# An edge-gated graph layer on one core: ScalarE's copies emitted ahead of the gate, and the low part of one product formed on TensorE

## Chip, core and metric

One core of a Trainium2 chip runs the whole layer in one launch. The metric is the device time of that launch in microseconds (us). The profile names the engines PE (TensorE; PEld is its weight load), DVE (VectorE), ACT (ScalarE), POOL (GpSimd) and SP (SyncE); the same names are used here.

## The reference, cut to what matters

```
B, C, D = 16, 1024, 256                       # batches, nodes, features
pre_u  = x @ W1[:D];  pre_v = x @ W1[D:]
S[b,u,v] = sigmoid( relu(pre_u[b,u] + pre_v[b,v] + b1) @ W2 + b2 )
a[b,v] = sum over u of S[b,u,v] * adj[u,v] * x[b,u]
m[b,v] = (sum over u of adj[u,v] * x[b,u]) * x[b,v]
z = beta1*x + beta2*(a @ Wa + ba) + beta3*(m @ Wm + bm)
```

`adj` is sparse (a few edges per node), so the kernel works edge by edge and not on the full square of nodes.

## The kernel before, in words

**Blocks and steps.** Batches are taken four at a time (four groups g), nodes v in tiles of 128 (eight tiles vt). A pair (g, vt) is a block; there are 32 blocks k, the last eight of them being the fourth group. A block has T = 10 steps s, two windows of 64 nodes with five steps of 128 edges each; step n is 10k + s, and there are 320. `table[g]` in DRAM holds, for each node u, `pre_u` and x of the group's four batches, 2048 numbers in all.

**What a step does.** `fetch` (L518, POOL queue) gathers 128 rows of the table into one of eight `fetched` buffers. `expand(n)` (L607, PE) spreads `pre_v + b1` of the block, held in `X`, over the 128 edges by two matmuls into `pc` (PSUM, two buffers). `add(n)` (L639, DVE) adds `pc` to the fetched `pre_u`. `gate(n)` (L647, DVE) makes relu and the product with W2 with its sum, four times, one for each batch; then ACT makes the sigmoid `gt` (L650) and four scaled copies `left` (L652), beside `left_adj` (L617). `aggregate(n)` (L664, PE) multiplies `left` with the fetched x and sums into `acc`. It is emitted two or three steps later, for two steps at once, in odd steps.

**What a block does beside it.** `products(n, k, s)` emits, by the step's number s in the block: `rows` (L459 to L465: `pre_u` for the table of a later group, with an ACT copy and an SP store); `turn_over` (L674: four transposes L682 of `ev`, an ACT copy L685 to `LT`, later the DVE product L696); `block_end` (L701: the last products L713 of the block before, in s = 4 to 7, an ACT copy L718 to `z` in s = 5 and 7, and a step later the DVE addition L719 and its store); and `halves` (L473) of the next block in s = 1, 3, 4, 6, 7. `halves` splits `pre_v + b1` in two parts that a reduced float32 (`FR`) can hold: ACT copies the PSUM tile `p` twice, to `X` rounded (L482) and to `low` whole (L483); DVE subtracts (L484); ACT writes the difference and a second copy of the high part into the free halves of `X` (L486, L489).

All products, transposes and `p` share one PSUM pool, `misc`, of two buffers: a third use waits until ACT has copied the one two before.

**The order is written by hand** (`manual_schedule`): each engine's queue runs in the order in which the loop from L860 emits. For n from ROOM = 10 on, a step emits: the aggregates that are due (with ACT's copy of a finished `acc` to `ev`, L672), the next `mark` (L550), `add(n+1)`, `gate(n)`, `left_adj(n+1)`, `do(n)`, `expand(n+2)`, the load of x for the output, `fill(n, False)`, `products(n)`. `do(n)` emits what was put off to step n by `after`: DVE's L484, L696 and L719, and SP's stores. `fill` emits one piece of the edge lists of later tiles (`lists`, ended by step 110). So on ACT the order in a step is

```
ev, mark, gt(n), left(n) x4, left_adj(n+1), copies of products(n)
```

and on PE it is aggregates, `expand(n+2)`, products(n).

Of the kernel before, what the change touches and what calls it, by code (L numbers as in the profile page):

```python
# [7 lines left out]
FP = mybir.dt.float32  # L8
FR = mybir.dt.float32r
I32 = mybir.dt.int32  # L10
AF = mybir.ActivationFunctionType
ALU = mybir.AluOpType
AX = mybir.AxisListType
P = 128
# [3 lines left out]
def kernel(  # L18
# [42 lines left out]
    nc = tc.nc  # L61
    B, N, D = x.shape
    NT = N // P
    DC = D // P
    GB = 4
    NG = B // GB
    GD = GB * D
    W = 64
    NW = P // W
# [31 lines left out]
    def fixed(shape, name, dt=FP):  # L101
        return const.tile(shape, dt, name=name)
# [9 lines left out]
    upto = fixed([P, E], "upto")  # L112
# [3 lines left out]
    row = rows32[:, 0:1]  # L116
# [56 lines left out]
    slot_of = fixed([P, NW, TW], "slot_of")  # L173
    for w in range(NW):
        nc.vector.tensor_scalar(slot_of[:, w, :], upto[:, :TW], float(P), row, ALU.mult, ALU.add)
    ident = fixed([P, P], "ident")
    nc.vector.tensor_scalar(ident, upto[:, :P], row, None, ALU.is_equal)
    place = upto[:, :W].rearrange("p (q v) -> p q v", v=V)
    slot, nth = upto, upto[:, :S]

# [11 lines left out]
    b1_p = fixed([P, D], "b1_p", FR)  # L192
# [16 lines left out]
    big = main.enter_context(tc.tile_pool(name="big", bufs=2))  # L209
# [10 lines left out]
    def small(name):  # L220
        return psm.tile([P, 512], FP, name="misc")
# [180 lines left out]
    def after(step, f):  # L402
        due.setdefault(step, []).append(f)
# [5 lines left out]
    order = [(g, vt) for some in (range(FIRST), range(FIRST, NT)) for g in range(2) for vt in some]  # L409
    again = [(g, vt) for g, vt in order if vt >= FIRST or g == 1]  # L410
    order += [(g, vt) for g in range(2, NG) for vt in range(NT)]
    hTs = {}
# [29 lines left out]
    def half_product(p, hT, wt, h, begun):  # L442
        for bb in range(2):
            for i in range(DC):
                nc.tensor.matmul(p[:, bb * D:(bb + 1) * D], hT[:, 2 * h + bb, i, :], wt[:, i, :],  # L445
                                 start=(i == 0 and not begun), stop=(i == DC - 1), skip_group_check=begun)

    def add_row(p, parts):
        nc.tensor.matmul(p, unit, parts.unsqueeze(1).to_broadcast([P, 2, D]),  # L449
                         start=True, stop=False, skip_group_check=True)  # L450
# [19 lines left out]

    cuts = {}

    def halves(k):  # L473
        X = cuts[k] = big.tile([P, NW, GD], FR, name="X")
        low = one.tile([P, GD], FP, name="low")
        for h in range(2):
            step = yield
            c = slice(2 * h * D, (2 * h + 2) * D)
            p = small("p")
            add_row(p, b1_p)  # L480
            half_product(p, hTs[order[k]], w_v, h, True)
            nc.scalar.copy(X[:, 0, c], p)  # L482
            nc.scalar.copy(low[:, c], p)  # L483
        after(step + (2 if k else 1), lambda: nc.vector.tensor_tensor(low, low, X[:, 0, :].bitcast(FP), ALU.subtract))  # L484
        yield
        nc.scalar.copy(X[W:, 1, :], X[W:, 0, :].bitcast(FP))  # L486
        for w in range(NW):
            yield
            nc.scalar.copy(X[(1 - w) * W:(2 - w) * W, w, :], low[w * W:(w + 1) * W])  # L489
# [5 lines left out]
    def do(step):  # L495
        for f in due.pop(step, ()):
            f()
# [8 lines left out]
    T = TW * NW  # L506

    BS = NG * NT

    def where(n):  # L510
        k, s = divmod(n, T)
        w, j = divmod(s, TW)
        return k, *order[k], w, j
# [20 lines left out]
    w_v = load_weights(W1[D:2 * D], "w_v", nc.sync)  # L534
# [11 lines left out]
    marks, pcs, accs, evs, hbs, LTs, lefts = {}, {}, {}, {}, {}, {}, {}  # L546
# [12 lines left out]
    parts = halves(0)  # L559
# [42 lines left out]
    def expand(n):  # L602
        k, g, vt, w, j = where(n)
        pcs[n] = psc.tile([P, GD], FP, name="pc")
        for h in range(2):
            c = slice(2 * h * D, (2 * h + 2) * D)
            nc.tensor.matmul(pcs[n][:, c], marks[n // TW][:, j * P:(j + 1) * P], cuts[k][:, w, c],  # L607
                             start=True, stop=True)
# [22 lines left out]
    def fill(n, gap=True):  # L631
        for r in running:
            if r[1] == gap and r[2] <= n:
                piece_of(r, n)
                break

    def add(n):
        t = fetched[at_slot[n]][:, :GD]
        nc.vector.tensor_tensor(t, t, pcs.pop(n), ALU.add)  # L639

    def gate(n):
        m = len(QUARTERS[n % TW])
# [157 lines left out]
    def products(n, k, s):  # L800
        nonlocal end, parts
        made_rows(n)
        if (s == 2 and 0 < k < BS) or n == total:
            turn_over(k - 1, 1, 1, n)
        z = 3 if n < ROOM else 4
        if z <= s < z + 4 and 0 < k < BS:
            if s == z:
                end = block_end(k - 1)
                next(end)
            go(end, n)  # L810
        if ROOM <= n < total - T:
            if s in (8, 9):
                turn_over(k, 0, s - 8, n)
        elif s == 7 and k < BS:
            turn_over(k, 0, 0, n)
        if s == 7 and k == BS - 1 or s == 8 and n < ROOM:
            turn_over(k, 0, 1, n)
        if (s == 0 and 0 < k < BS) or n == total - 1:
            turn_over(k - (s == 0), 1, 0, n)
        if n == total - 2:  # L820
            end = tail(tails[:2], n)
            next(end)
        elif n == total - 1:
            go(end, n)
        elif n >= total:
            end = tail([tails[2 + n - total]], n)
            next(end)
            go(end, n)
            go(end, n)
        later = n >= ROOM  # L830
        if k + 1 < BS and s - later in (0, 2, 3, 5, 6):
            if s == later:
                parts = halves(k + 1)
                next(parts)
            go(parts, n)

# [3 lines left out]
    total = BS * T  # L840
    ROOM, MORE, LISTS = 10, 3, 110
    ahead = NF
    add(0)

    def refill():
# [14 lines left out]
    for n in range(total + 2):  # L860
        k, s = divmod(n, T)
        if n < total - 3:
            last_in = n - 1 if n % 2 or n < ROOM else done
        else:
            last_in = n
        while done < min(last_in, total):
            gather_in(done)
            done += 1
        if n % TW == 1 and n // TW + 1 < total // TW:
            load_mark(n // TW + 1)  # L870
        if n < ROOM:
            if n + 2 < total:
                expand(n + 2)
            products(n, k, s)
        if n + 1 < total:
            add(n + 1)
        if n < total:
            gate(n)
            if n + 1 < total:
                left_adj(n + 1)  # L880
        do(n)
        if n >= ROOM and n + 2 < total:
            expand(n + 2)
        if n == 1:
            w_a = load_weights(Wa, "w_a", nc.sync)
            w_m = load_weights(Wm, "w_m", nc.sync)
            bias = load_rows(bm, D, "bias", nc.sync, spare[:, 1])
            ba_b = load_rows(ba, D, "ba_b", nc.sync, spare[:, 2])
            be1 = load_rows(beta1, 1, "be1", nc.sync)
            be2 = load_rows(beta2, 1, "be2", nc.sync)  # L890
            be3 = load_rows(beta3, 1, "be3", nc.sync)
            after(10, scale_late)
        if s in (5, 7) and k < BS - 1:
            h = s // 7
            hb = big.tile([P, 2, D], FP, name="h_blk", bufs=4)
            hbs.setdefault(k, []).append(hb)
            g, vt = order[k]
            nc.sync.dma_start(hb.rearrange("p b d -> p (b d)"),
                              table[g][vt * P:(vt + 1) * P, GD + 2 * h * D:GD + (2 * h + 2) * D])
        if n == total - 6:  # L900
            hbs[BS - 1] = hT_free.pop(0).rearrange("p b c n -> p b (c n)")
            for v, m, f in tails:
                for h, o in tail_rows(x, v, m, f):
                    nc.sync.dma_start(h, o)
        for i in advance.get(n, ()):
            next(made[i], None)
        if n in start_list:
            running.append([made[start_list[n]], True, n])
            piece_of(running[-1], n)
        fill(n, False)  # L910
        if n >= ROOM:
            products(n, k, s)
        if n == LISTS:
            assert not running and all(next(x, None) is None for x in made)
            lists_done()
            more = main.enter_context(tc.tile_pool(name="more", bufs=1))
            hT_free.extend(hT_places(more, MORE, NH))
        if n == 120:
            nc.gpsimd.partition_all_reduce(longest, rest, P, bass_isa.ReduceOp.max)
            after(n + 12, count_rest)  # L920
# [7 lines left out]
    with tc.If(any_left > 0):  # L928
        with ExitStack() as s2:
# [4 lines left out]
            for vt in range(NT):  # L934
# [55 lines left out]
                for b in range(B):  # L990
# [7 lines left out]
                    for k, w in enumerate((w_m, w_a)):  # L998
                        for c in range(DC):
                            nc.tensor.matmul(pz, lt[:, k, c, :], w[:, c, :],  # L1000
                                             start=(k == 0 and c == 0), stop=(k == 1 and c == DC - 1))
# [34 lines left out]
```

## Time and profile before

| | us |
|---|---|
| three runs | 1098.24, 1101.68, 1102.35 (median 1101.68) |
| profiled execution, device time | 1101.12 |
| its span, first to last instruction | 1099.3 |
| PE, DVE, ACT busy | 1022.2, 1025.4, 872.5 |
| add of step 10 to add of step 120 (blocks 1 to 11) | 101.4 to 483.3: 34.7 a block |
| add of step 120 to add of step 230 (blocks 12 to 22) | 483.3 to 819.5: 30.56 a block |
| add of step 230 to add of step 310 (blocks 23 to 30) | 819.5 to 1050.4: 28.86 a block |

The stages are read from the starts of the additions L639 in the timeline: there are 320, one a step. "Busy" of PE counts a matmul until its modelled end; consecutive matmuls overlap, and the chain of waits is the better guide to what a matmul takes in a stream. The number after an "idle before" or in the list of waits is time in which an engine stood, and the name behind the arrow is what let it go on.

### The profile page before, as it was taken

Reading aid. Unit: us, or ns where it says so; the run is one execution under the profiler, and the core shown is the slowest. Engines: PE = TensorE matmul, PEld = TensorE weight load, DVE = VectorE, ACT = ScalarE, POOL = GpSimd, SP = SyncE. Lnnn points to the kernel's source line nnn. Section 1 sums busy time; section 2 is a strip of 40 time slices with the busy share of each in tenths; the row PEclk is TensorE's granted clock in tenths of the full one; section 3 lists DMA queues with packets and bytes.
Section 4 is the critical chain, followed back from the end, with each engine's and each line's share of the span. In section 5 each row is a group of like instructions: output and inputs, shape, how many; then the busy total and the mean of one; then the engine's idle time right before and its main releaser. Section 6 shows DMA issues by size and latency. Waiting matters only on the chain.

```text
span 1099.3 us, 23917 instructions
## 1 busy us (share of the span) xinstructions
PE 1022.2 (93%) x7645; PEld 726.5 (66%) x7645; DVE 1025.4 (93%) x3487; ACT 872.5 (79%) x2616; POOL 464.3 (42%) x453
## 2 busy tenths in 40 slices
PE   7777889999899999999999999999999999999986
PEld 6654556776667666676777677767766666666653
DVE  8788888898999999999999999999999999999994
ACT  3347667787778888888988889888889888888873
POOL 2746575445347433563334343433343333333330
PEclk9988989999899999999999999999999999999999
DMA  9999799999999999999999999999999999999991
GB/s 285 331 391 311 295 327 303 356 394 382 384 343 344 391 410 381 384 378 396 408 382 400 406 400 398 386 398 388 353 362 383 372 350 357 359 372 363 354 335 42
DMA packets 149030, 394.54 MB, mean 359 GB/s; under 512 B 18224, under 2 KB 96048, under 8 KB 112688
## 3 DMA queue, kind: packets, MB, share of 16 engines
q0 software_dynamic: 50240, 300.11, 69.6%
q1 hardware_dynamic: 85360, 79.71, 22.9%
q10 hardware_dynamic: 13296, 13.11, 3.6%
q8 instruction: 62, 1.02, 0.3%
q14 instruction: 72, 0.59, 0.1%
HBM read 396.93 MB, written 50.33 MB: 407 GB/s over the span
## 4 chain that ended last, share of the span: by engine, by line
PE 39%; DVE 32%; issue 10%; ACT 9%; DMA 6%; POOL 2%; another core or an unknown queue 0%; SPq 0%; POOLq 0%; DVEq 0%; ACTq 0%
DVE fetched L647 15%; DVE fetched L639 12%; PE acc L664 10%; PE misc L713 10%; PE misc L445 7%; PE pc L607 7%; ACT left L652 3%; PE misc L682 2%; DMA hT<-in_xT_dram 2%; DMA hT<-in_x_dram 2%; PE misc L449 1%; DMA fetched<-table,uidx 1%; DVE low L484 1%; DVE h_blk L719 1%; DVE LT L696 1%
## 5 line engine op out<-in xcount | busy, mean ns | idle before, releaser
L518 POOL DMA_INDIRECT fetched<-table,uidx x320 | 345.5, 1080 | 540.9 <-PE acc L664 384.1
L647 DVE SCALAR_TENSOR_TENSOR fetched<-fetched,w_b 128x256 f32<-128x256 f32 x1280 | 476.5, 418 | 0.0
L639 DVE TENSOR_TENSOR fetched<-fetched,pc 128x1024 f32<-128x1024 f32 x320 | 387.9, 1212 | 38.1 <-PE pc L607 23.1
L652 ACT ACTIVATE left<-left,gt 128x32 f32<-128x32 f32 (+1 forms) x1280 | 299.5, 304 | 10.4
L664 PE MATMUL acc<-fetched,left 128*32 128x256 f32 x4096 | 271.7, 390 | 5.9 <-ACT left L652 4.6
L607 PE MATMUL pc<-X,mark 128*128 128x512 f32 x640 | 245.9, 466 | 12.1 <-DVE fetched L639 12.0
L664 PEld LDWEIGHTS acc<-fetched,left 128*32 128x32 f32 x4096 | 123.7, 111 | 113.1 <-issue 38.8
L650 ACT ACTIVATE gt<-sc,b_b 128x4 f32<-128x4 f32 x320 | 95.5, 298 | 94.8 <-DVE fetched L647 84.4
L607 PEld LDWEIGHTS pc<-X,mark 128*128 128x128 f32 x640 | 106.3, 191 | 91.8 <-issue 48.9
L713 PE MATMUL misc<-w_a,LT 128*128 128x256 f32 x496 | 118.7, 383 | 0.0
L713 PE MATMUL misc<-w_m,LT 128*128 128x256 f32 x496 | 117.2, 379 | 0.0
L445 PE MATMUL misc<-w_v,hT 128*128 128x256 f32 x448 | 108.1, 385 | 1.0 <-DMA hT<-in_xT_dram 1.0
L682 PE MATMUL misc<-ident,ev 128*128 128x128 f32 x512 | 81.3, 282 | 27.0 <-ACT low L483 9.3
L713 PEld LDWEIGHTS misc<-w_a,LT 128*128 128x128 f32 x496 | 94.7, 191 | 15.7 <-issue 0.4
L713 PEld LDWEIGHTS misc<-w_m,LT 128*128 128x128 f32 x496 | 93.9, 189 | 15.2
L617 ACT ACTIVATE left<-onehot,val 128x64 f32<-128x64 bf16 (+1 forms) x320 | 102.9, 322 | 0.0
L385 POOL DMA_INDIRECT val<-in_adjT_dram,vidx x80 | 87.6, 1095 | 33.2 <-issue 18.9
L647 DVE DVE_READ_ACCUMULATOR fetched<-fetched,w_b 128x1 f32 x1280 | 100.4, 78 | 0.0
L682 PEld LDWEIGHTS misc<-ident,ev 128*128 128x128 f32 x512 | 61.2, 143 | 55.1 <-ACT low L483 14.7
L445 PEld LDWEIGHTS misc<-w_v,hT 128*128 128x128 f32 x448 | 86.6, 194 | 16.0 <-DMA hT<-in_xT_dram 1.9
L672 ACT COPY ev<-acc 128x512 f32<-128x512 f32 x128 | 74.7, 584 | 15.4 <-PE acc L664 6.8
L685 ACT COPY LT<-misc 128x512 f32<-128x512 f32 x128 | 73.1, 572 | 5.6 <-PE misc L682 2.9
(178 smaller groups left out, 974.6 us busy)
## 6 DMA issues: line engine op xcount, KB each, us to landing
h_blk<-table SPq DMA_DIRECT2D x62, 256.0 KB
out_dram<-h_blk SPq DMA_DIRECT2D x62, 256.0 KB
hT<-in_xT_dram SPq DMA_DIRECT2D x28, 512.0 KB
table<-in_x_dram ACTq DMA_DIRECT2D x24, 512.0 KB
table<-tab SPq DMA_DIRECT2D x48, 256.0 KB
fetched<-table,uidx POOLq DMA_INDIRECT x320
table<-in_x_dram SPq DMA_DIRECT2D x8, 512.0 KB
table<-fetched SPq DMA_DIRECT2D x8, 512.0 KB
```

The lines of the kernel that those rows point to most:

```text
L385: nc.gpsimd.indirect_dma_start(out=val[:, i, j:j + 1], out_offset=None, in_=adj_flat, in_offset=bass.IndirectOffsetOnAxis(ap=vidx[:, i, j: ...
L445: nc.tensor.matmul(p[:, bb * D:(bb + 1) * D], hT[:, 2 * h + bb, i, :], wt[:, i, :], start=(i == 0 and not begun), stop=(i == DC - 1), skip ...
L518: nc.gpsimd.indirect_dma_start(out=fetched[at_slot[n]], out_offset=None, in_=table[g], in_offset=bass.IndirectOffsetOnAxis(ap=uidx[:, vt * ...
L607: nc.tensor.matmul(pcs[n][:, c], marks[n // TW][:, j * P:(j + 1) * P], cuts[k][:, w, c], start=True, stop=True)
L617: nc.scalar.activation(lefts[n][:, :m, 1::GB, :], onehot[:, i, o:o + m, :].unsqueeze(2).to_broadcast([P, m, GB // 2, V]), AF.Copy, scale=v ...
L639: nc.vector.tensor_tensor(t, t, pcs.pop(n), ALU.add)
L647: nc.vector.scalar_tensor_tensor(t[:, b, :], t[:, b, :], 0.0, w2_b, ALU.max, ALU.mult, accum_out=sc[:, b:b + 1])
L650: nc.scalar.activation(gt, sc, AF.Sigmoid, bias=b2_b)
L652: nc.scalar.activation(lefts[n][:, :m, 2 * b, :], lefts[n][:, :m, 1 + b // 2 * GB, :], AF.Copy, scale=gt[:, b:b + 1])
L664: nc.tensor.matmul(accs[h][b * 2 * V:(b + 1) * 2 * V, r, :], left[:, i, 2 * b - b % 2:2 * b - b % 2 + 2].rearrange("p k v -> p (k v)"), f[ ...
L682: nc.tensor.transpose(pt[:, r, :, c, :], ev[:, r, c * P:(c + 1) * P], ident)
L713: nc.tensor.matmul(pz[:, bb * D:(bb + 1) * D], LTs[k][:, 2 * h + bb, i if bb else 1 - i, c, :], wt[:, c, :], start=False, stop=(i == 0 and ...
```

## The change

For every step from 10 to 309, `expand(n+2)`, `fill(n, False)` and `products(n)` are emitted ahead of `add(n+1)`, `gate(n)` and `left_adj(n+1)`. The last block's ten steps keep the old order. On ACT a step is now

```
ev, mark, copies of products(n), gt(n), left(n) x4, left_adj(n+1)
```

PE's order (aggregates, `expand`, products) stays. `do(n)` stays behind the gate, with one exception: in s = 8 it runs ahead of `products(n)`, because `turn_over` takes a new `LT` there and the addition L719, which reads `z` out of the old `LT`, has to be emitted before. So in s = 8 DVE does L719 first, then `add(n+1)` and `gate(n)`.

For the eight blocks of the last group (`turned`), `halves` is replaced by `halves_turned`, in s = 1 to 4 (two steps for each half). ACT writes minus the rounded product to `X`, PE adds that to `p` through an identity matmul, and what is left in `p` is the low part; ACT writes it, negated, to `X`. The DVE subtraction L484 goes, and since `X` now holds the negative, `add` subtracts.

```
+    def halves_turned(k):
+        X = cuts[k] = big.tile([P, NW, GD], FR, name="X")
+        for h in range(2):
+            yield
+            c = slice(2 * h * D, (2 * h + 2) * D)
+            p = small("p")
+            add_row(p, b1_p)
+            half_product(p, hTs[order[k]], w_v, h, True)
+            nc.scalar.activation(X[:, 0, c], p, AF.Copy, scale=-1.0)
+            nc.scalar.copy(X[W:, 1, c], X[W:, 0, c].bitcast(FP))
+            yield
+            nc.tensor.matmul(p, ident_r, X[:, 0, c], start=False, stop=True, skip_group_check=True)
+            for w in range(NW):
+                nc.scalar.activation(X[(1 - w) * W:(2 - w) * W, w, c], p[w * W:(w + 1) * W], AF.Copy, scale=-1.0)
...
-        nc.vector.tensor_tensor(t, t, pcs.pop(n), ALU.add)
+        nc.vector.tensor_tensor(t, t, pcs.pop(n), ALU.subtract if turned(n // T) else ALU.add)
...
-        if k + 1 < BS and s - later in (0, 2, 3, 5, 6):
+        if k + 1 < BS and s - later in (range(4) if turned(k + 1) else (0, 2, 3, 5, 6)):
             if s == later:
-                parts = halves(k + 1)
+                parts = (halves_turned if turned(k + 1) else halves)(k + 1)
...
-        if n < ROOM:
-            if n + 2 < total:
-                expand(n + 2)
+        if n < total - T:
+            expand(n + 2)
+            if n >= ROOM:
+                fill(n, False)
+                if s == 8:
+                    do(n)
             products(n, k, s)
...
         do(n)
-        if n >= ROOM and n + 2 < total:
+        if n >= total - T and n + 2 < total:
             expand(n + 2)
...
-        fill(n, False)
-        if n >= ROOM:
+        if n < ROOM:
+            fill(n, False)
+        if n >= total - T:
             products(n, k, s)
```

`turned(k)` is true for k from 24 on; `ident_r` is the identity matrix in the reduced type, and the transposes read the same bytes as before.

More of the change, by code (lines that the diff above doesn't have):

```diff
@@ L175 @@
         nc.vector.tensor_scalar(slot_of[:, w, :], upto[:, :TW], float(P), row, ALU.mult, ALU.add)
-    ident = fixed([P, P], "ident")
-    nc.vector.tensor_scalar(ident, upto[:, :P], row, None, ALU.is_equal)
+    ident_r = fixed([P, P], "ident_r", FR)
+    nc.vector.tensor_scalar(ident_r, upto[:, :P], row, None, ALU.is_equal)
+    ident = ident_r.bitcast(FP)
     place = upto[:, :W].rearrange("p (q v) -> p q v", v=V)
@@ L471, with turned @@
     cuts = {}
+    def turned(k):
+        return k >= NT * (NG - 1)
+    def halves_turned(k):
[12 more added lines that the diff above has]
+                nc.scalar.activation(X[(1 - w) * W:(2 - w) * W, w, c], p[w * W:(w + 1) * W], AF.Copy, scale=-1.0)
     def halves(k):
```

## The prediction

> **What bounds the kernel now.** I read the page's totals first, then the busy table by stretches, because totals average over stages.
>
> ```profile
> PE 1022.2 (93%) x7645; PEld 726.5 (66%) x7645; DVE 1025.4 (93%) x3487; ACT 872.5 (79%) x2616; POOL 464.3 (42%) x453
> ...
> 580.00:660.00 80.00, 78.22 (x606) 56.57 (x599) 77.11 (x254) 69.34 (x211) 29.30 (x26) 1.00 1.02 401
> ...
> 820.00:900.00 80.00, 77.60 (x612) 53.39 (x608) 80.00 (x266) 70.89 (x221) 28.51 (x28) 1.00 0.98 378
> 900.00:980.00 80.00, 76.40 (x605) 52.16 (x599) 80.00 (x265) 71.46 (x221) 28.59 (x28) 1.00 0.96 359
> ```
>
> Columns of a stretch: length, busy PE, PEld, DVE, ACT, POOL, granted clock, DMA share, GB/s. In the middle (blocks 12 to 22) PE is busy 78.2 of 80, DVE 77.1, and DMA carries 401 GB/s at a share of 1.02: three resources near their end. From 820 on (blocks 23 to 30) DVE never stops. Which wait decides in the middle is told by the chain of waits:
>
> ```profile
> 614.20 0.63 ACT mark L550
> 614.82 0.21 ACT gt L650
> 615.05 0.96 ACT left L652 x4
> 616.01 0.24 ACT left L617
> 616.25 0.47 ACT X L482
> 616.72 0.49 ACT low L483
> 617.21 0.04 issue
> 617.25 0.66 PE misc L682 x4
> 617.91 1.43 PE acc L664 x24
> ```
>
> Once a block PE stands for the copies of `X` and `low`: its transposes (L682) need the `misc` buffer that `low` is read from, and ACT does `gt`, four `left` and `left_adj` first. The rest of the block's chain is PE.
>
> The third view is the timeline at s = 7 and 8, for two blocks: step 168 begins at 632.78, step 288 at 989.50.
>
> ```profile
> 632.58 1.89 PE L713 MATMUL misc<-w_m,LT 128*128 128x256 f32 x8
> 632.78 1.22 DVE L639 TENSOR_TENSOR fetched<-fetched,pc 128x1024 f32<-128x1024 f32 x1
> 634.51 0.59 ACT L718 COPY LT<-misc 128x512 f32<-128x512 f32 x1
> 635.30 0.74 DVE L719 SCALAR_TENSOR_TENSOR h_blk<-h_blk,be,LT 128x512 f32<-128x512 f32 x1
> ...
> 987.53 1.89 PE L713 MATMUL misc<-w_m,LT 128*128 128x256 f32 x8
> 989.50 1.21 DVE L639 TENSOR_TENSOR fetched<-fetched,pc 128x1024 f32<-128x1024 f32 x1
> 991.04 0.56 ACT L718 COPY LT<-misc 128x512 f32<-128x512 f32 x1
> 992.01 0.74 DVE L719 SCALAR_TENSOR_TENSOR h_blk<-h_blk,be,LT 128x512 f32<-128x512 f32 x1
> ```
>
> L719 of s = 8 now comes at the step's end, after `z` (L718) in both blocks. The change puts it at the step's start, 632.78 and 989.50, and there `z` is not ready: PE's last product ends at 634.47 and 989.42.
>
> [...] the ready copy of `X` waits behind `left`. [...] The trace has 572 to 584 ns for 128x512 and 0.47 to 0.49 from start to start. [...] the trace has 1212 (`add`) and 1248 (L484). [...] the chain is used below for what PE's work takes.
>
> **Step 1, the order on ACT, middle stage.** Nothing is added. The copies no longer wait for the gate. Ahead of `X` and `low` went `gt`, `left` and `left_adj` (0.21 + 0.96 + 0.24 = 1.4); without them both are done before PE asks (PE stood 0.58 there), and `ev` comes up to 0.3 earlier. `left(n)` now waits for the copies instead. PE needs it two steps later, and ACT's sum is the same, so I cost that at nothing; if that cover went, it would be the 0.97 of two copies a step. The list pieces and ACT's DMA issues (0.56 each, L439) move ahead of the gate with them; SP's loads of hT pass ahead of SP's stores. Their data are used several steps later: nothing.
>
> **Step 2, the wait that s = 8 adds.** DVE's L719 stands first in s = 8 and waits for `z`; behind it in DVE's queue are `add` and the gate of s = 8 and 9, then `left(9)`, then PE's aggregate of s = 1. That closes a loop from `z` to the next block's `z`:
> - DVE: L719 0.67, then two steps of 2.52 (add 1.13 to 1.14, four L647 of 0.345 from start to start): 5.71.
> - ACT: gt and four `left`: 0.30 + 0.96 + 0.11 of handing over = 1.37.
> - PE from the chain, second half of the aggregates of s = 1 to the products of s = 7: 0.47 + 0.66 + 1.96 + 0.46 + 1.73 for s = 1 and the start of s = 2, then 0.44 (transposes without their wait) and 617.91 to 634.47 = 16.56: 22.3.
> - ACT's copy of `z` with its handing over: 0.68.
>
> Sum 30.06. PE's own work in a block is about 29.6 (30.56 less the 0.95 that it stands), DVE's 28.9 (25.2 for ten steps, 1.14 for L484, 1.3 for two L719, 1.2 for two L696). So the loop is the longest: **30.1 against 30.56**, 0.46 x 11 blocks = **5.1 less**. DMA must move the same bytes in 1.5% less time at a share of 1.02; I expect it to, since the page's best slice moved 410 GB/s, but take 5.0 and keep 1.5 as the lower end.
>
> **Step 3, the last group.** Per block this removes L484 (1.14 on DVE), two copies of `low` (2 x 0.48) and three of 64x1024 (3 x 0.93) on ACT, and adds two identity matmuls and six 64x512 copies. The trace has neither form. The matmul: between 0.23 (the row matmul L449, 512 columns in the same type, in the chain) and its 0.42 alone; I take 0.23. The copy: 64x1024 takes 1.045 and 128x1024 1.06 (L255), so partitions hardly count and a 64x512 copy should take 0.48, at most 0.58. ACT's share of this is 4 x 0.48 + 3 x 0.93 = 4.7 before and 8 x 0.48 = 3.8 after: ACT is not the bound.
>
> If DVE alone decided, the block would go from 28.86 to 27.7. But the loop of step 2 holds here too. PE has no L445 for a table (1.73 less) and two identity matmuls (0.46 more). In s = 2 the first of these waits for `X` of s = 1, behind `ev` and `mark` on ACT, and `left(1)` is last there (the list has eight waits of PEld for L652 of 0.4 already): 0.75 together, between 0 and 0.9. So 5.71 + 1.37 + (22.3 - 1.73 + 0.46 + 0.75 = 21.8) + 0.68 = **29.55**, 28.8 without any wait. A check from the other side: at 989.50 DVE would have waited for a `z` that ends at 990.03, 0.53, though it had done L484. So 0.69 x 8 = **5.5 more**, between 0 and 7; what DVE saves turns into a wait for `z`.
>
> **Step 4, blocks 1 to 11.** In the stretch from 95 to 480 PE's list of waits for ACT's copies adds up to 15.3 (LT 4.3, low 3.8 and 3.6, tab 1.5, z 1.4 and 0.7). These are what the new order shortens. But list pieces keep DVE at 77 to 78 of 80 from 340 to 500, so PE's gain can't be passed on there. I take **4.0 less**; ends 15.3 less, or a loss (rival D). Steps 0 to 9 and the last block keep their order: 0, ends 1 either way.
>
> **Sum:** -5.0 + 5.5 - 4.0 = -3.5. The profiled execution's 1101.12 becomes **1097.6**; the median, 1101.68, lies 0.6 above that execution, which I leave out.
>
> **Rivals.**
> A, the forecast, 1097.6: chance 0.42.
> B, DVE's saving counts: PE gets ahead enough for `z` to be there, 8 x 1.14 = 9.1 less: 1101.1 - 5 - 4 - 9.1 = 1083. For it: DVE is busy 80 of 80. Against: the PE path above. 0.13.
> C, the early waits all go: 1101.1 - 15.3 - 5 + 5.5 = 1086.3. For it: they are named ACT copies. Against: DVE's lists. 0.16.
> D, **slower**: the wait for `z` also binds in blocks 6 to 11. In the timeline the end of PE's last product plus 0.6 lies after the start of s = 8 by 2.3, 1.6, 1.9, 0, 1.85 and 2.2: 9.85. If list pieces leave DVE no room to regain it, that is added, the early gain is nil, the middle gains 1.5 for DMA: 1101.1 + 9.85 - 1.5 + 5.5 = 1115. It decides from the point at which DVE's idle time in such a block (2 or less there) is smaller than the wait. Half of it gives 1110. 0.24.
> E, the new order does nothing, because ACT was seldom late: 1101. 0.05.
>
> **Numbers.** About 0.5%, 5.5 us, is what a measurement of this kernel can tell from no change. A spreads some 5 either way: 0.105 of it is faster by more, 0.02 slower. Faster: 0.105 + 0.13 + 0.15 of C = 0.385, 0.38. Slower: 0.02 + 0.20 of D = 0.22. Same: 0.40. The range 1084 to 1110 leaves out about half of B and less than half of D.
>
> **What would show it.** Step 1: PE's waits for L483 in the middle vanish, a block takes 30.1. Step 2: a new wait of L719 for ACT's L718, once a block, about 1 in the middle. Step 3: the same wait at 1.5 to 2 in the last group, DVE no longer at 80 of 80, blocks of 29.5; blocks of 27.7 would show B. Step 4: blocks 1 to 11 sum to 378 against 381.9; above 388 is D, below 370 is C. The forecast is wrong if L719 waits for nothing, or if ACT's `left` becomes PE's main wait.

## The result, and the profile after

| | before | after |
|---|---|---|
| median of 22 runs each, same chip, us | 1102.41 (1097.48 to 1118.46) | 1104.67 (1096.49 to 1114.20) |
| ratio, 95% interval | | 1.0024 [1.0006, 1.0042] |
| profiled execution, device time (span) | 1101.12 (1099.3) | 1107.99 (1106.2) |
| blocks 1 to 11 in it | 381.9 | 379.5 |
| blocks 12 to 22 in it, a block | 30.56 | 30.14 to 30.22, block 17 30.47 |
| blocks 23 to 30 in it, a block | 28.86 | 30.47 to 30.51 |

The change makes the kernel 0.24% slower; the forecast was 0.4% faster. The ratio leaves out the slow runs, those more than 1.5% above the fastest of their kernel (two before, one after). The stages are again read from the starts of the additions, now L658. Against before, the middle gives 4.1 us (332.1 against 336.2) and the last group costs 13.0 (243.9 against 230.9). The two regular stages repeat from block to block within 0.1, but for block 17. Blocks 1 to 11 don't: in the profiled execution one of them, block 4, took 39.75, because ACT stood 8.7 us for a load of `hT`. None of six other executions with this order had that wait, though some had another of its kind (in e3 ACT stood up to 7.7 us for a store out of `tab`). So that stage is better taken from medians, further down.

The page's totals and the line of the group that changed most, with the line of the same group in the kernel before (L719) under it; then the same stretches as before:

```profile
PE 1034.2 (93%) x7661; PEld 740.1 (67%) x7661; DVE 1013.9 (92%) x3479; ACT 857.5 (78%) x2624; POOL 466.6 (42%) x453
...
L738 DVE SCALAR_TENSOR_TENSOR h_blk<-h_blk,be,LT 128x512 f32<-128x512 f32 x62 | 46.3, 746 | 40.3 <-ACT LT L737 40.3
...
L719 DVE SCALAR_TENSOR_TENSOR h_blk<-h_blk,be,LT 128x512 f32<-128x512 f32 x62 | 46.1, 744 | 0.0
```

```profile
580.00:660.00 80.00, 79.52 (x606) 58.30 (x605) 75.89 (x250) 69.04 (x212) 29.30 (x26) 1.00 1.02 395
...
900.00:980.00 80.00, 74.81 (x572) 51.74 (x570) 72.76 (x245) 65.31 (x209) 28.14 (x28) 1.00 0.93 342
```

DVE has 11.5 us less work than before (1013.9 against 1025.4), and the addition of `z` (L719, now L738) has 40.3 us of idle time ahead of it, where the kernel before had 0.0. In the middle PE rises from 78.2 to 79.5 of 80. In the last group DVE falls from 80.00 to 72.76, and PE from 76.4 to 74.8: neither engine is full there any more, and the granted clock is 1.00. This points to a chain that runs from engine to engine.

The timeline at the same two steps, 168 and 288 (`z` is L737 now):

```profile
628.95 0.59 ACT L737 COPY LT<-misc 128x512 f32<-128x512 f32 x1 [0.16 <-PE misc L732]
629.57 0.75 DVE L738 SCALAR_TENSOR_TENSOR h_blk<-h_blk,be,LT 128x512 f32<-128x512 f32 x1 [1.29 <-ACT LT L737]
...
962.61 0.59 ACT L737 COPY LT<-misc 128x512 f32<-128x512 f32 x1 [1.35 <-PE misc L732]
963.23 0.75 DVE L738 SCALAR_TENSOR_TENSOR h_blk<-h_blk,be,LT 128x512 f32<-128x512 f32 x1 [2.38 <-ACT LT L737]
```

L738 now comes ahead of the addition of pc (L658, next at 630.24 and 963.90), and DVE stands for it (the number in brackets): 1.29 us in the middle, 2.38 in the last group. The chain of waits shows one turn of the loop in the last group, from an addition of s = 8 to the next `z` (start, length):

```profile
963.90 1.21 DVE fetched L658
...
974.17 0.50 ACT X L485
974.69 0.62 ACT X L486
975.34 0.31 ACT gt L669
975.66 0.33 ACT left L671
976.04 1.69 PE acc L683 x15
977.73 0.66 PE pc L626 x2
...
991.33 1.74 PE misc L732 x8
993.09 0.60 ACT LT L737
...
994.38 1.21 DVE fetched L658
```

Three parts: DVE and ACT (three steps of addition and gate, then `gt`, `left`, `ev`, `mark` and the lines shown) up to the aggregate of s = 3 and its `expand`, 963.90 to 977.73 = 13.83; PE without a pause from there to the end of the last products, 15.34; `z` and the addition, 1.31. Sum 30.48, the block. The stretch to look at is 974.17 to 975.66: two copies to `X` stand in ACT's queue ahead of the gate whose `left` PE is waiting for.

### The profile page after: what moved, and what is told of

Same layout as the page of the kernel before. It is cut to its first block, busy times and chain, and to the rows that moved or that the text cites. A ratio compares the mean times of both kernels' runs of the same rounds, so it can differ in the third digit from the quotient of the medians.

```text
span 1106.2 us, 24129 instructions
## 1 busy us (share of the span) xinstructions
PE 1034.2 (93%) x7661; PEld 740.1 (67%) x7661; DVE 1013.9 (92%) x3479; ACT 857.5 (78%) x2624; POOL 466.6 (42%) x453
## 4 chain that ended last, share of the span: by engine, by line
PE 54%; DVE 20%; ACT 11%; DMA 8%; issue 5%; POOL 1%; SPq 0%; ACTq 0%; DVEq 0%; POOLq 0%
PE misc L732 15%; PE misc L446 13%; PE acc L683 13%; PE pc L626 8%; DVE fetched L666 8%; DVE fetched L658 7%; ACT left L671 3%; DMA hT<-in_xT_dram 3%; DMA fetched<-table,uidx 3%; PE misc L701 2%; PE misc L450 2%; ACT LT L737 1%; ACT X L508 1%; ACT gt L669 1%; DMA key<-in_adjT_dram 1%
## 5 line engine op out<-in xcount | busy, mean ns | idle before, releaser
L658 DVE TENSOR_TENSOR fetched<-fetched,pc 128x1024 f32<-128x1024 f32 x320 | 387.6, 1211 | 15.4 <-PE pc L626 6.6
L671 ACT ACTIVATE left<-left,gt 128x32 f32<-128x32 f32 (+1 forms) x1280 | 299.6, 305 | 10.4
L683 PE MATMUL acc<-fetched,left 128*32 128x256 f32 x4096 | 281.4, 388 | 11.9 <-ACT left L671 11.8
L626 PE MATMUL pc<-X,mark 128*128 128x512 f32 x640 | 245.4, 465 | 25.8 <-DVE fetched L658 24.1
L683 PEld LDWEIGHTS acc<-fetched,left 128*32 128x32 f32 x4096 | 133.2, 110 | 120.6 <-issue 28.8
L626 PEld LDWEIGHTS pc<-X,mark 128*128 128x128 f32 x640 | 106.2, 191 | 106.8 <-issue 44.7
L701 PE MATMUL misc<-ident_r,ev 128*128 128x128 f32 x512 | 80.2, 280 | 7.9 <-ACT tab L462 2.3
L701 PEld LDWEIGHTS misc<-ident_r,ev 128*128 128x128 f32 x512 | 62.0, 143 | 34.9 <-ACT ev L691 15.7
L738 DVE SCALAR_TENSOR_TENSOR h_blk<-h_blk,be,LT 128x512 f32<-128x512 f32 x62 | 46.3, 746 | 40.3 <-ACT LT L737 40.3
## 6 DMA issues: line engine op xcount, KB each, us to landing
out_dram<-h_blk SPq DMA_DIRECT2D x62, 256.0 KB, 10.2
table<-in_x_dram SPq DMA_DIRECT2D x8, 512.0 KB, 11.5
```

What stands on the lines that cost most here:

```text
L658: nc.vector.tensor_tensor(t, t, pcs.pop(n), ALU.subtract if turned(n // T) else ALU.add)
L671: nc.scalar.activation(lefts[n][:, :m, 2 * b, :], lefts[n][:, :m, 1 + b // 2 * GB, :], AF.Copy, scale=gt[:, b:b + 1])
L683: nc.tensor.matmul(accs[h][b * 2 * V:(b + 1) * 2 * V, r, :], left[:, i, 2 * b - b % 2:2 * b - b % 2 + 2].rearrange("p k v -> p (k v)"), f[ ...
L701: nc.tensor.transpose(pt[:, r, :, c, :], ev[:, r, c * P:(c + 1) * P], ident)
```

## The experiments

The theory: the addition of `z`, put first in s = 8, closes a loop that is longer than DVE's work, and what ACT now does ahead of `left` lengthens it in the last group. The main rival (T in the expectations): the turned halves themselves are what makes the last group longer. Unless said otherwise, each edit is made in the changed kernel; all of them compute the whole layer. A ratio is to runs of the kernel before on the same chip.

**e1: the order alone.** `turned` gives False, so that the last group has the old halves with the DVE subtraction.

```
     def turned(k):
-        return k >= NT * (NG - 1)
+        return False
```

> Theory L (a loop): in the last group ACT's copies of X stand ahead of left of s = 1, which PE waits for, and the z of s = 7 is waited for by DVE at the start of s = 8; together they close a loop of 30.5 us. Here the old halves makes two 128x512 copies (0.96) in that place instead of 0.50 + 0.62, and one identity matmul less on PE counts (0.23): a block of the last group takes 30.1, the middle 30.15 as in the changed kernel, and the time is about 3 us under the changed kernel, some 1101. Rival T (the turned halves itself is too dear): without it the last group goes back to 28.9 and the time to about 1091. Rival D (DMA holds the last group): no change, 30.5.

Median 1101.69 over 20 runs, 0.9992 [0.9965, 1.0019] of the kernel before. Middle 30.15, last group 29.92. So the order alone, with the early addition of `z` that belongs to it, costs 1.06 a block in the last group (29.92 less 28.86), 8.5 us in eight; on top of it the turned form adds another 0.57, 4.6 us. The rival that gives the order no part in it falls. The list of waits, from 805 to 1045 (us in total, times, longest):

```profile
PE acc L683 <- ACT left L671: 9.4, 16, 0.7
...
DVE h_blk L738 <- ACT LT L737: 7.9, 8, 1.0
```

PE stands 9.4 us for `left` (L671), and DVE stands 7.9 for `z`: with the old halves too, the copies (`X` and `low`, 0.48 + 0.49 in its chain) are on the path. The granted clock is 1.00 here, as in the changed kernel, so it has no part in the 1.06.

**e2: the low part alone.** Old order in every step, turned halves in the last group.

```
-        if n < total - T:
+        ahead_ = False
+        if n < ROOM or ahead_:
             expand(n + 2)
-            if n >= ROOM:
+            if ahead_:
                 fill(n, False)
...
-        if n >= total - T and n + 2 < total:
+        if n >= ROOM and not ahead_ and n + 2 < total:
             expand(n + 2)
...
```

> The old order everywhere, the turned halves in the last group. Theory L: no copy stands ahead of left and no z is waited for, so DVE alone decides: 28.86 less 1.14 for the subtraction is 27.7 a block in the last group, at most 28.0 with small waits; middle 30.56; the time is 7 to 9 us under the kernel before, about 1094. Rival T: the last group takes 29.5 or more, the time 1107 or more. Rival D: 28.9, as before.

Median 1111.15 over 4 runs, 1.0129 [1.0049, 1.0208]; seven of the eight blocks of the last group take 30.5, the last one 29.25. My expectation was too low by 2.5 a block in the seven, and taken by itself this is the number of the rival. Its chain of waits names another cause than the loop through `z`, however; under it stands PE's timeline at the same place:

```profile
916.82 0.49 ACT X L485
...
917.35 0.50 PE misc L488
917.85 2.30 PE acc L683 x24
920.15 1.15 PE pc L626 x2
...
917.35 0.50 PE L488 MATMUL misc<-X,ident_r 128*128 128x512 f32 x1 [1.88 <-ACT X L485]
```

In the old order `X` is copied behind the gate, and the identity matmul (L488) that needs it is early in PE's next step: PE stands 1.88 there, in each of eight blocks (15.0 in its list of waits). After it, 24 matmuls of the aggregate take 2.30 where they take 1.43 elsewhere, and two of `expand` 1.15 instead of 0.66: the granted clock of TensorE, 1.00 from 914.00 to 917.30, was 0.63 from there to 921.00.

**e3: the order for steps 10 to 229, the old one with turned halves from 230.**

```
-        if n < total - T:
+        ahead_ = ROOM <= n < 230
+        if n < ROOM or ahead_:
             expand(n + 2)
...
```

> The new order for steps 10 to 229 alone, the turned halves with the old order from step 230. Theory L: middle 30.15 as in the changed kernel, last group 27.7 to 28.0: 4.5 + 8 and some 4 in the early blocks, about 16 us under the kernel before, 1086; 1090 if the early blocks give nothing. Rival T: last group 29.5 or more, time 1100. Rival D: last group 28.9, time 1094.

Median 1102.46 over 20 runs, 0.9985 [0.9960, 1.0009]. Middle 30.15 (one block 31.1); the last group has two kinds of block, three of 29.26 and five of 30.51. That is the rival's number again, and the same failure as in e2, but with its two parts apart. Here are two blocks by the busy table, a stretch each (columns as before; the granted clock is the third number from the end):

```profile
902.20:932.70 30.50, 28.62 (x222) 20.07 (x218) 27.96 (x95) 25.30 (x81) 10.07 (x10) 0.94 0.91 328
932.70:961.96 29.26, 27.30 (x222) 18.99 (x218) 27.89 (x95) 25.31 (x81) 10.06 (x10) 1.00 0.95 351
```

A block whose clock stays at 1.00 takes 29.26, one in which it falls to 0.94 takes 30.51, though PE stands the same 1.88 in both. e2 shows the same: 0.94 in its seven long blocks and 1.00 in the last. So of the 1.65 that e2 loses against 28.86, 1.25 is the clock; the other 0.40 is PE's standing for `X`, less whatever the missing subtraction gives. Even at the full clock the block is 1.3 above the expectation, which had left this standing out. The turned halves without the new order gain nothing, and the new order without them doesn't either: in the last group each part alone makes the block longer. In the old order, then, the rival is right; whether it is right in the new one, e4 and e7 decide.

**e4: `z` in a tile of its own from step 230.** The last group doesn't use the tile `low`; the copy L737 of the second half goes there, `turn_over` no longer needs the addition out of its way, and `do(8)` goes back behind the gate.

```
+                if h == 1 and 230 <= step < total - T:
+                    z = one.tile([P, GD], FP, name="low")[:, :2 * D].rearrange("p (b d) -> p b d", b=2)
...
-                if s == 8:
+                if s == 8 and n < 230:
                     do(n)
```

> The changed kernel, but from step 230 on z of s = 7 goes to the tile that low no longer uses, and the deferred work of s = 8 stays at the end of the step. Theory L: DVE no longer waits for z; what is left of the loop ends at the expand of s = 7, ahead of its products, 1.73 + 0.6 earlier: 28.2 a block of the last group, middle 30.15, time 18 us under the changed kernel, about 1086. Rival T or D: the last group stays at 30 or more. If only the order of ACT's copies counted and not the wait for z, it stays at 29.7 to 30.5 too.

Median 1087.24 over 4 runs, 0.9865 [0.9822, 0.9909]; the last group takes 28.1 to 28.4 (one block 28.7). Taking the wait for `z` away gives 2.1 to 2.4 a block, so the last group did stand on it. This is the experiment that settles between the loop and the turned halves in the new order: they are all still there.

**e5: only the early addition, in the kernel before.** Nothing else of the change.

```
+        if s == 8 and ROOM <= n < total - T:
+            do(n)
         if n + 1 < total:
             add(n + 1)
```

> The kernel before, with one thing of the change: in s = 8 of steps 10 to 309 the deferred work (L719, which reads z) is emitted ahead of the addition. Theory L: z is copied at 991.60 in the trace of before where step 8 begins at 989.50, so DVE stands 2.1 us once a block and the last group takes 28.86 + 2.1 = 31.0; in the middle the loop through z, 30.1 and PE's stall for the copies of 0.6, gives 30.6 to 30.9. If DVE regains the wait, both stages stay as they were, 28.9 and 30.56.

1141.91, one run; middle 31.65, last group 31.0. Its list of waits for the last group, 830 to 1090, has the new wait:

```profile
DVE h_blk L719 <- ACT LT L718: 18.9, 9, 2.4
```

The last group is as expected, the middle 0.8 above the expectation's upper end. The added wait by itself costs 1.1 a block in the middle and 2.1 in the last group. The granted clock fell here too (0.963 over the run, where 15 runs of the kernel before had 0.971 to 0.980), to 0.94 or less in seven of the last eight blocks, but block 23, where it is 1.00, takes 31.0 like the others, so the clock isn't what makes them long. In the middle the new order on ACT more than repays it (31.65 to 30.15); in the last group it repays less (31.0 to 29.92).

**e6: the second copy of the high part a step later.** L486 moves behind the second `yield`.

```
             nc.scalar.activation(X[:, 0, c], p, AF.Copy, scale=-1.0)
+            yield
             nc.scalar.copy(X[W:, 1, c], X[W:, 0, c].bitcast(FP))
-            yield
             nc.tensor.matmul(p, ident_r, X[:, 0, c], start=False, stop=True, skip_group_check=True)
```

> The changed kernel, but the copy of the high part to the other half of X (64x512, 0.62) is emitted a step later, behind the gate of its step. Theory L (ACT's copies ahead of left of s = 1 lie on the loop): the last group goes from 30.49 to 29.9, 5 us off the changed kernel, about 1099.5. If those copies are beside the path, it stays at 30.5.

Median 1095.96 over 12 runs, 0.9959 [0.9926, 0.9992]; last group 29.72, 0.77 less than with the change as it is. The same copies, one of them (0.62) moved out of the way of `left`: ACT's work is unchanged, the block is shorter. So the copies ahead of `left` are on the path.

**e7: e4 and e6 together.**

> e4_z_beside and e6_second_copy_later together. With the wait for z gone the chain of e4 runs over PE and, twice a block, over ACT's two copies ahead of left; one of them out of the way takes up to 0.62 twice, and DVE's 27.7 is the floor: 27.7 to 27.9 a block in the last group, 4 us under e4_z_beside, about 1083. If the copies are beside the path, 28.3 as in e4.

Median 1081.51 over 4 runs, 0.9801 [0.9747, 0.9856]; last group 27.72.

```profile
820.00:900.00 80.00, 80.00 (x627) 57.61 (x625) 80.00 (x273) 71.53 (x233) 29.71 (x29) 1.00 0.97 368
```

DVE is full again, with a block 1.14 shorter than before: just the subtraction that the change removes. This is the number of the prediction's rival B, reached once the two waits are gone.

**e8: e7, and a tile for `z` from step 117 on.** One of the buffers for x transposed (`hT`) is given up for its room.

```
-    ROOM, MORE, LISTS = 10, 3, 110
+    ROOM, MORE, LISTS = 10, 2, 110
...
+                if h == 1 and 117 <= step < total - T:
+                    z = z_apart[0].tile([P, 2 * D], FP, name="z").rearrange("p (b d) -> p b d", b=2)
...
-                if s == 8:
+                if s == 8 and n < 118:
                     do(n)
```

> e7_both, and from step 117 on z of s = 7 has a tile of its own in the middle stage too (one buffer of hT less), with the deferred work of s = 8 at the end of its step. Theory L: the middle loses the wait for z and PE's own work decides, 29.6 to 29.7 instead of 30.15: about 5 us under e7_both, 1078. If DMA holds the middle (share 1.02 before), it stays at 30.1 in blocks 12 to 18.

Median 1078.61 over 4 runs, 0.9791 [0.9723, 0.9859]: the lowest, though its interval overlaps that of e7. Blocks 11 and 12 take 29.2, but 13 to 22 take 30.1 on average, where 29.6 to 29.7 was expected for the whole stage. DVE no longer waits for `z` there. What took its place is in the chain (block 19):

```profile
651.62 0.59 ACT z L739
...
652.23 1.05 ACT X L508
...
655.77 0.21 ACT gt L669
...
657.18 0.48 ACT ev L691
...
657.70 0.66 PE misc L701 x4
```

ACT works from 651.62 to 657.66 with no gap over 0.04 (`z`, `X`, gate and `left` of one step, `tab`, `LT`, gate and `left` of the next, `ev`), and PE's transposes (L701) wait for `ev` at the end of it: in the middle a second loop, through ACT's queue, is about as long as the one through `z`. DVE waits 0.2 us for DMA in that stage, so DMA isn't seen to be the bound. That ACT's queue is the cause is read from the chain and was not tried by another run; nor was the loss of one `hT` buffer tried alone.

## Why the prediction was wrong

The sum had -5.0 for the middle, +5.5 for the last group and -4.0 for blocks 1 to 11. Measured: -4.1, +13.0 and, as the rest of the 2.3 between the medians, -6.6. (In the profiled execution, with its long block 4, blocks 1 to 11 give only -2.4.)

**Step 2 (the wait in s = 8): right, in its size partly by luck.** 30.06 was forecast for the loop, 30.15 measured. The list of waits of the middle, from 480 to 814:

```profile
DVE h_blk L738 <- ACT LT L737: 13.9, 11, 1.6
```

The same list of the kernel before, from 480 to 819, had none of it, and instead:

```profile
PEld misc L682 <- ACT low L483: 9.9, 11, 1.1
...
PE misc L682 <- ACT low L483: 5.7, 9, 0.7
```

DVE waits for `z` once in each of 11 blocks, 1.26 on average where about 1 was forecast, and PE's waits for `low` are gone: step 1 held for the middle. The loop runs differently from the way I wrote it, through ACT's gate to `ev` and PE's transposes and not through `left(9)`. From `z` to PE the chain takes 5.8 us (629.55 to 635.38) where I had 7.1 (5.71 + 1.37), and PE then takes 23.7 where I had 22.3. The two differences nearly cancel; that is luck.

**Step 3 (the last group): the step that failed.** The mechanism is the one named: what DVE saves becomes a wait for `z`. Its size was not. For PE's standing at the identity matmul and at `left(1)` I took "0.75 together, between 0 and 0.9". PE's timeline in the same turn of the loop:

```profile
973.27 0.81 PE L626 MATMUL pc<-X,mark 128*128 128x512 f32 x2
...
974.72 0.49 PE L488 MATMUL misc<-X,ident_r 128*128 128x512 f32 x1 [0.19 <-ACT X L485]
975.14 0.64 PE L683 MATMUL acc<-fetched,left 128*32 128x256 f32 x8
976.04 1.69 PE L683 MATMUL acc<-fetched,left 128*32 128x256 f32 x16 [0.26 <-ACT left L671]
977.66 0.73 PE L626 MATMUL pc<-X,mark 128*128 128x512 f32 x2
```

From 973.27 to 977.66 are 4.39 us. The work in it, at the durations that these have in the chain, is 0.46 (`expand`) + 0.44 (transposes) + 0.23 (identity) + 1.43 (24 of the aggregate) = 2.56. PE loses **1.83** and not 0.75. Only 0.45 of that shows as idle (0.19 + 0.26). The last 16 matmuls, which follow `left` one by one, take 1.69, where 16 of them take 1.00 in the chain at 989.67; the rest lies in the overlap of the stream (the identity matmul starts 0.42 ahead of what follows it, where the chain has 0.23 for it at 982.76). Ahead of this stretch the forecast was right: from the addition at 963.90 to 973.27 its terms give 9.50, and the trace has 9.37. The part of the loop from the addition to the `expand` of s = 3 is 13.83 where the forecast's own terms give 12.8; the rest of the loop is 0.1 shorter than forecast, and 30.48 less 29.55 is 0.93. Times eight, 7.4 of the 7.5 that the last group is off.

Why the term was too small is in **step 1**: "`left(n)` now waits for the copies instead. PE needs it two steps later ... so I cost that at nothing; if that cover went, it would be the 0.97 of two copies a step." In the last group the cover is gone. There PE doesn't run ahead of DVE; it waits for DVE's addition to free `pc` (8.0 us in 814 to 1057), and with it for each `left`. In the turned form the two copies are 0.50 + 0.62 = 1.12, `ev` and `mark` are ahead of them, and `left(1)` comes last. e1 shows this cost with the old halves (1.06 a block in all), e6 takes 0.77 of it back with one copy moved. I had the price and named the cover, and named `left` as PE's main wait as a sign of being wrong (in the last group it is PE's second wait, 2.0 us of idle time in 814 to 1057 behind the 8.0 for DVE's addition; the idle time shows a part of the loss only). But I carried the cover from the middle over to a stage where PE has another place in the loop.

A smaller miss of the same step: a copy of 64x512 was taken at 0.48, at most 0.58; L486 takes 0.62 and L490 0.59.

**Step 4 (blocks 1 to 11): the sign right, the size about, the cause open.** In six comparisons of medians with the kernel before, the difference less what the two regular stages give leaves -4.4 to -7.7, mean -6.4, for the change and e1, e3, e4, e6 and e7; this contains the start and the last block. PE's waits for ACT's copies fell from 15.3 to 10.2 in the profiled execution, of which 5.7 is the load of `hT` in block 4. Some of it came back as waits of PE for DVE's addition (L626 for L658, 6.0 against 0.4 before), as the busy DVE had let expect. One more thing was not in the sum: the granted clock. In block 6 it was 0.86 in the kernel before, and in e2, whose order is the old one, and the block took 36.0 in both. In the changed kernel and the six others with its order it was 1.00 there, and the block took 33.5 to 33.7. Over blocks 1 to 11 the mean clock is 0.96 before and 0.98 after. Whether fewer stalls of PE brought this about wasn't tried, and these runs don't allow a finer split.

**The rivals.** B, 27.7 in the last group, did not happen (30.5); e7 shows what it takes. C took all 15.3 us of early waits as gained: apart from block 4 about 11 of them did go, but the medians give 6.4. D came in part: the addition of `z` does wait in blocks 6 to 11, but 3.7 us in three of them, where D had 9.85. And these blocks together take 195.0 against 195.9, because 6 to 9 became 4.8 shorter while 10 and 11 became 3.8 longer (one execution each). So the kernel became slower, but in the last group, and not by D's sum. E falls with the middle.

## What to carry to other kernels

Ready work moved ahead of a gate in an engine's queue was free here only where the consumer of that gate was behind; check this in each stage, because the same order, with the early addition that it forces, was worth 0.4 us a block in one stage here and cost 1.1 in the next. When an operation leaves the busiest engine, write out the loop that the remaining waits close, through all engines, before counting its time as saved: here a buffer shared with `z` turned the saved 1.14 us a block into a wait of 2.4. A spare tile in place of an order that a shared tile forces, and one copy moved by a step, made of the same change a kernel at 0.980 of the time before, and not 1.0024.

## What the runs showed of the hardware

**In e2 the granted clock was lower behind a stall of PE.** PE stood 1.88 us, up to 917.35. The two stretches behind that stall:

```profile
917.30:921.00 3.70, 3.65 (x27) 1.90 (x28) 3.70 (x14) 3.58 (x10) 1.56 (x2) 0.63 0.98 379
921.00:925.00 4.00, 4.00 (x18) 3.36 (x18) 3.67 (x11) 2.96 (x10) 0.92 (x1) 0.92 0.94 360
```

The granted clock was 0.63 for 3.7 us and 0.92 for 4.0: 1.69 us of full clock lost. From 925.00 to 935.00 it was 1.00 again. It fell behind a stall of 1.88 in seven of eight blocks of e2's last group and in five of eight of e3's. Why not in all of them, these runs don't show. In the changed kernel, whose standing of 1.83 is spread over several matmuls, the clock stayed at 1.00 through the last group.

**Half the partitions didn't make a copy on ACT shorter.** 64x512 took 0.59 from PSUM, 128x512 from PSUM 0.56 to 0.60; 64x512 from SBUF took 0.62. The half copies were even dearer in the queue: two of L490, one behind the other, took 1.19. Copies of 128x512 that follow one another start every 0.47 to 0.49, 0.1 before the one ahead has ended. L486 began only after L485 had ended (974.07 + 0.59, start at 974.69). It reads what L485 wrote; but the 64x1024 copy L508, which reads nothing of the copy of `z` ahead of it, also began 0.02 after its end, in each of the 11 blocks of the middle. And `left`, of full height, never began before the end of `gt`, which it reads (0.03 after it, in each of the 320 steps). So either may cost the overlap, and which of the two it was for L486 isn't shown.
